# A graph layer's projection on raw rows, its weights loaded by other queues, six row groups instead of five, and a bias added behind the attention

## The chip, the cores and the metric

The kernel runs on one core of a Trainium2 chip, as one program and one launch. A core has five engines with their own instruction queues: TensorE (PE; its loads of the stationary operand are shown as PEld), VectorE (DVE), ScalarE (ACT), GpSimd (POOL) and SyncE (SP). SP, ACT and POOL also issue DMAs. Each engine takes its instructions in order; engines wait for each other by semaphores. The metric is the device time in microseconds, from start to end of the program on the core.

## The reference, cut to what matters

Two layers, each a graph attention over 3327 nodes followed by a feed-forward part. Layer 0's feed-forward part is a mixture of 16 experts of which each row takes two; layer 1's is 30 recurrent steps. The change concerns layer 0's graph attention with 2 heads of 128 features:

```python
x = x + L0_gnn(layernorm(x), adj, W1, b1, W2, b2, W3, b3, a)
x = x + L0_experts(layernorm(x), ...)          # top 2 of 16 experts
x = x + L1_gnn(layernorm(x), adj, W, a)        # one head of 256, elu
x = x + L1_recurrent(layernorm(x), ...)        # 30 steps

def L0_gnn(h, adj, W1, b1, W2, b2, W3, b3, a):
    W1h, W2h, W3h = h @ W1.T + b1, h @ W2.T + b2, h @ W3.T + b3     # (n, 2, 128)
    s1, s2 = W1h . a[:, :128], W2h . a[:, 128:]                     # (n, 2)
    e = leaky_relu(s1[:, None] + s2[None, :], 0.2)
    att = softmax(where(adj == 1, e, -9e15), axis=1)
    return att @ W3h                                                # per head
```

## The kernel before, in words

**State and tiles.** x lies in SBUF as 26 tiles of 128 rows by 256 features for the whole program. Lines 94 and 95 load it with SP in groups of 4 tiles. The adjacency is kept as bytes, turned (`adjT`): the column tile's 128 nodes lie on the partitions, the rows along the free axis.

**Taking the graph.** `take_graph` (L286) does that for one group of rows: POOL issues a DMA that casts the group's int32 rows to bytes in DRAM (`in_bytes`, L301), and SP issues one transposing DMA per tile into `adjT` (L311). There is one `in_bytes` buffer of 6 tiles, so the next group's cast waits until the transposes before it have read it.

**Projection of layer 0** (L387 to L456). POOL loads W1, W2, the attention vectors `aT`, the three biases and W3 (L400, L412), in this order. Sixteen one-column matmul records (L415) turn W1 and W2 with `aT` into four extra columns of the weight `wv`, which is 256 + 4 columns wide, so that one product gives the features and the scores. `project` (L151) then goes over the rows in groups of 4 tiles: statistics on VectorE (`inverse`, L109: bn_stats, bn_aggr), 1/sqrt on POOL (L120), normalised rows `xn` on VectorE (L127), four transposes for two tiles on TensorE (L147) with a copy to SBUF on ScalarE (L148), and the products of the two tiles before (L162). `split0` (L433) adds b3 to the features and a constant to the scores on VectorE; `Scores.finish` (L193) takes exponentials of the scores on ScalarE. Layer 1 calls the same function with raw rows: the mean is taken out of the weights (`without_mean`, L132) and 1/sigma is applied to the product (`split1`, L923).

**Attention** (`attend`, L201). For each group of rows, for each of 2 heads, for each of the 26 column tiles j: ScalarE makes `e` (L252) for all rows of the group, VectorE adds and multiplies with the mask into `pT` (L257), and TensorE adds one product for each row tile to `acc` (L262). `e` and `pT` have three buffers each. The row factors `rb` of the next part are made half way (L221, L225). The groups of rows are `groups0` (L45). When a group's head is done, `close` divides by the sum and adds into x (L235, L479) in small steps, one for each j of the next part. After the second head the generator `route` (L486) follows in the same way: normalise the group's rows into `row` (L490), store them, multiply with the gate, find the best two experts and their places, and queue the tokens' scattered DMAs (`list_tokens`, L565), each of which may also start the graph for a later group (L578). After the third group `find_tiles` (L631) finds which rows the first 16 slots of the experts work on.

**Experts.** `work_off` (L797) runs 61 slots; each loads an expert's weights by SP and gathers 128 rows by POOL. The routing of the last group runs beside the first slots.

**Order.** The framework's scheduler plans the order of each engine's queue when the program is built, from the order of the code and the dependencies; the transposes of `row` thus stand at a fixed place in TensorE's queue between products of the attention. `tc.issue_after` and `tc.keep_in_program_order` tie instructions to others.

Of the kernel before, what the change touches and what calls it, by code (L numbers as in the profile page):

```python
# [20 lines left out]
P = 128  # L21
# [4 lines left out]
G = 4  # L26
# [4 lines left out]
def gat_moe_gat_recurrent_ffn(ctx: ExitStack, tc: tile.TileContext, a: dict, out: bass.AP):  # L31
# [12 lines left out]
    groups = [range(t, min(t + G, NT)) for t in range(0, NT, G)]  # L44
    groups0 = [range(0, 4), range(4, 10), range(10, 16), range(16, 22), range(22, 26)]  # L45
    groups1 = [range(max(t - 2, 0), t + 2) for t in range(0, NT, G)]
# [46 lines left out]

    for ts in groups:
        move_pairs(a["x"], x[:, ts[0] : ts[-1] + 1, :], ts[0] // 2, (ts[-1] + 1) // 2, False)

# [35 lines left out]
    def without_mean(wv, n_out, ones, p):  # L132

        for k in range(KD):
            nc.tensor.matmul(p[:, :n_out], lhsT=ones, rhs=wv[:, k, :], start=(k == 0), stop=(k == KD - 1))
        for k in range(KD):
            nc.vector.scalar_tensor_tensor(
                wv[:, k, :], p[:, :n_out], -1.0 / D, wv[:, k, :], op0=ALU.mult, op1=ALU.add
            )

    def turned(two, work, ps):
# [8 lines left out]

    def project(groups, wv, n_out, finish, work, ps, ps_p, aside, raw=True):  # L151

        pending = None

        def products(hT, t, r):
            for j in range(2):
                p = ps_p()  # L160
                for k in range(KD):
                    nc.tensor.matmul(  # L162
                        p[:, :n_out], lhsT=hT[:, j, k, :], rhs=wv[:, k, :], start=(k == 0), stop=(k == KD - 1)
                    )
                finish(t + j, p, *([r[:, j : j + 1]] if raw else []))

        for ts in groups:
            n = len(ts)
            tiles = [x[:, t, :] for t in ts]
            if raw:  # L170
                r, _, power = inverse(tiles)
            else:
                xn = work.tile([P, G, D], F32, name="xn")
                power = normalized(tiles, [xn[:, j, :] for j in range(n)])
            aside(ts, power)
            for j0 in range(0, n, 2):
                hT = turned(x[:, ts[j0] : ts[j0] + 2, :] if raw else xn[:, j0 : j0 + 2, :], work, ps)
                if pending:
                    products(*pending)
                pending = hT, ts[j0], r[:, j0 : j0 + 2] if raw else None  # L180
        products(*pending)

    class Scores:


        def __init__(self, pool, heads, s=None):
            self.s = pool.tile([P, NT, 2, heads], F32, name="s") if s is None else s
            self.row = pool.tile([P, NT, heads], F32, name="row")
            self.full = pool.tile([P, NT, heads], F32, name="full")
            self.part = pool.tile([P, NT, heads], F32, name="part")  # L190
            self.minus = pool.tile([P, NT, heads], F32, name="minus")

        def finish(self, t0, t1):  # L193
            nc.scalar.activation(self.full[:, t0:t1], self.s[:, t0:t1, 1], AF.Exp)
            nc.scalar.activation(self.part[:, t0:t1], self.s[:, t0:t1, 1], AF.Exp, scale=ALPHA)
            nc.scalar.activation(self.row[:, t0:t1], self.s[:, t0:t1, 0], AF.Exp, scale=1.0 - ALPHA)
            nc.vector.tensor_scalar(self.minus[:, t0:t1], self.part[:, t0:t1], -1.0, None, op0=ALU.mult)
# [133 lines left out]
    lb = rec.tile([P, KD], F32, name="lb")  # L331
    fb = rec.tile([P, D], F32, name="fb")
    ones_r = rec.tile([P, P], F32, name="ones_r")
# [24 lines left out]
    with ExitStack() as moe:  # L358
# [19 lines left out]
        wh = keep.tile([P, NT, H, C + 1], F32, name="wh")  # L378
        sc = Scores(keep, H)
        ps = moe.enter_context(tc.tile_pool(name="ps0", bufs=4, space=PSUM))  # L380
# [6 lines left out]
        with ExitStack() as pre:  # L387
            work = pre.enter_context(tc.tile_pool(name="work0", bufs=2))
            hold = pre.enter_context(tc.tile_pool(name="hold0", bufs=1))

            zero = hold.tile([P, E * CAP * 2 // P], F32, name="zero")
            nc.vector.memset(zero, 0.0)
            nc.scalar.dma_start(lists.rearrange("(p n) k -> p (n k)", p=P), zero)
            for k in range(2):
                nc.scalar.dma_start(given[k * NP + N : (k + 1) * NP, :], zero[: NP - N, :D])
            nc.scalar.dma_start(no_row, zero[:2, : NP // 4])

            def once(name, shape, src):
                t = hold.tile(shape, F32, name=name)
                nc.gpsimd.dma_start(t, src)  # L400
                return t

            w1 = once("gw1", [P, H, D], a["W1"].rearrange("(h c) d -> c h d", c=P))
            w2 = once("gw2", [P, H, D], a["W2"].rearrange("(h c) d -> c h d", c=P))
            aT = once("gaT", [P, 2, H], a["aT"].rearrange("(s c) h -> c s h", c=P))
            b1 = once("gb1", [P, H], a["b1"])
            b2 = once("gb2", [P, H], a["b2"])
            b3 = once("gb3", [P, D], every_partition(a["b3"], D))


            wv = hold.tile([P, KD, D + 2 * H], F32, name="wv")
            nc.gpsimd.dma_start(wv[:, :, :D], a["W3T"].rearrange("(k p) c -> p k c", p=P))  # L412
            pv = bank()
# [7 lines left out]
            )  # L421
            shift = hold.tile([P, 2, H], F32, name="shift")
            nc.vector.memset(shift, 0.0)
            pv = bank()
            for h in range(H):
                for s, b in ((0, b1), (1, b2)):
# [3 lines left out]
                    )  # L430
            nc.vector.tensor_copy(shift[:, 0, :], pv[:, :H])

            def split0(t, p):  # L433
                nc.vector.tensor_tensor(
                    wh[:, t, :, :C], p[:, :D].rearrange("p (h c) -> p h c", h=H),
                    b3.rearrange("p (h c) -> p h c", h=H), ALU.add,
                )
                nc.vector.tensor_tensor(
                    sc.s[:, t], p[:, D : D + 2 * H].rearrange("p (s h) -> p s h", h=H), shift, ALU.add
                )  # L440
                if t % G == G - 1 or t == NT - 1:
                    sc.finish(t - t % G, t + 1)
# [5 lines left out]
            def first_rows(ts, power):  # L448
                nonlocal behind
                behind = power  # L450
                if ts is groups[3]:
                    take_graph(groups0[0], behind)

            project(groups, wv, D + 2 * H, split0, work, ps, bank, first_rows, False)
            nc.vector.tensor_scalar(wh[:, NT - 1], wh[:, NT - 1], real[:, 0:1], None, op0=ALU.mult)
# [30 lines left out]
        def route(ts):  # L486

            n, t0 = len(ts), ts[0]
            whole = [P, n, E]
            normalized([x[:, t, :] for t in ts], [row[:, j, :] for j in range(n)])  # L490
            here = slice(t0 * P, (t0 + n) * P)
# [72 lines left out]
            def list_tokens(j, t, s, behind):  # L564
                put = nc.gpsimd.indirect_dma_start(  # L565
                    out=lists, out_offset=bass.IndirectOffsetOnAxis(ap=ati[: rows(t), s, j : j + 1], axis=0),
                    in_=pair[: rows(t), t, s, :], in_offset=None,
                )
                tc.declare_no_dep(put.ins, group="places", reason="no two tokens have the same place in the lists")
                tc.add_to_no_dep_group("places", put.ins)  # L570
                if behind:

                    tc.add_manual_dep(
                        put.ins, behind.name,
                        mybir.DependencyInfo(mybir.DependencyClass.Sync, mybir.DependencyReason.DATA),
                        reason="spread over the columns",
                    )
                if (t, s) == (ts[-1], 1) and groups0.index(ts) < 2:  # L578
                    take_graph(groups0[groups0.index(ts) + 3], put.ins)

            for j, t in enumerate(ts):
                for s in range(2):
                    later.append(partial(list_tokens, j, t, s))
            if ts is groups0[2]:
                pieces = begin_tiles()

                def piece(behind):
                    if next(pieces, pieces) is not pieces:
                        later.appendleft(piece)

                quick.append(piece)
                later.append(piece)
# [4 lines left out]
        FIRST = 16  # L597
        EARLY = groups0[2][-1] + 1
        assert EARLY < NT - 1 and (2 * P * EARLY - E * (P - 1)) / P >= FIRST
# [271 lines left out]
        wc = rec.tile([P, KD, D], F32, name="wc")  # L871
        bb = rec.tile([P, D], F32, name="bb")
        wv1 = rec.tile([P, KD, D + 2], F32, name="wv1")
        va = rec.tile([P, 2, D], F32, name="va")
# [204 lines left out]
```

The softmax here doesn't subtract the row's maximum and nothing guards it: scores larger than these inputs give would overflow.

## Time and profile before

| | us |
|---|---|
| median of 3 runs | 2000.29 (1998.33 to 2000.75) |
| the profiled execution | 2004.62 |
| its span | 2002.9 |
| TensorE busy (matmul / weight load) | 1930.9 / 1750.0 |
| VectorE, ScalarE, GpSimd busy | 1299.7, 1095.5, 938.4 |

The span falls into five stages by the lines that run on TensorE: loads and layer 0's projection (0 to 53.3 us), its attention (53.3 to 395), the experts (to about 750), layer 1's projection and attention (to about 1100), and the recurrent steps. The page's groups show how often the lines of this change run: the attention's products (L262) leave 2704 records of 128x129 in layer 0 and 1352 of 128x257 in layer 1, the e and pT operations 494 each over both layers, 260 of them in layer 0. A busy TensorE in the profile is not TensorE at its peak, since the ends of matmuls are modelled; counts of records in equal windows are the better measure.

### The profile page before, as it was taken

The page shows a single profiled execution, that of the slowest core. Times are in us where ns is not written, and L with a number is a line of the kernel's source. Part 1 is how long each engine was busy: PE and PEld are TensorE (multiplying, and loading weights), DVE is VectorE, ACT ScalarE, POOL GpSimd, SP SyncE. Part 2 cuts the span into 40 slices and gives each one's busy share as a digit, 9 for nine tenths or more (in the row PEclk, how much of TensorE's full clock was granted, in tenths as well). Part 3 has the DMA queues.
Part 4 walks back from the last instruction along what each step waited for, and adds up shares of the span by engine and source line. Part 5 has one row for each costly group of instructions (what it writes and reads, how often), then busy time and mean ns, then how long its engine had stood idle before and what let it go on. Part 6 is the DMA issues. An engine that isn't in the chain of part 4 may idle for free.

```text
span 2002.9 us, 33524 instructions
## 1 busy us (share of the span) xinstructions
PE 1930.9 (96%) x12032; PEld 1750.0 (87%) x12032; DVE 1299.7 (65%) x3827; ACT 1095.5 (55%) x1419; POOL 938.4 (47%) x864
## 2 busy tenths in 40 slices
PE   7999999999999997999999999999999999999998
PEld 6999999989999986888888888888888888888887
DVE  6887888722222226567576777777777777777777
ACT  2967766621111115566555666666666666666664
POOL 3020212443333321001000787787787787787785
PEclk9999999999999998999999999999999999999999
DMA  8978141189999854000001000000000000000003
GB/s 165 119 100 119 10 76 50 39 291 324 351 330 308 297 195 137 9 8 17 9 17 35 1 1 1 1 1 1 1 1 1 1 1 1 1 1 1 1 1 116
DMA packets 139754, 157.08 MB, mean 78 GB/s; under 512 B 52027, under 2 KB 99364, under 8 KB 139586
## 3 DMA queue, kind: packets, MB, share of 16 engines
q1 hardware_dynamic: 123466, 122.05, 19.8%
q0 software_dynamic: 11440, 28.09, 8.1%
q10 hardware_dynamic: 4680, 4.76, 0.7%
q8 instruction: 98, 1.61, 0.3%
q14 instruction: 70, 0.57, 0.1%
HBM read 164.58 MB, written 29.78 MB: 97 GB/s over the span
## 4 chain that ended last, share of the span: by engine, by line
PE 68%; issue 9%; ACT 5%; POOL 5%; DVE 4%; DMA 3%; SPq 0%; another core or an unknown queue 0%; POOLq 0%; DVEq 0%; ACTq 0%
PE po L1014 35%; PE acc L262 23%; PE pt L1008 5%; ACT zT L1010 5%; DVE pT L257 2%; POOL given L831 2%; POOL rb L730 2%; DMA given<-wh,to 2%; PE bank L786 2%; PE acc L827 1%; PE bank L499 1%; PE bank L221 0%; DVE x L913 0%; PE acc L162 0%; POOL rstd L120 0%
## 5 line engine op out<-in xcount | busy, mean ns | idle before, releaser
L1014 PE MATMUL po<-wc,zT 128*128 128x256 f32 x3120 | 705.5, 383 | 21.7 <-ACT zT L1010 21.1
L1014 PEld LDWEIGHTS po<-wc,zT 128*128 128x128 f32 x3120 | 583.1, 190 | 124.1 <-ACT zT L1010 49.7
L252 ACT ACTIVATE e<-rb,minus,full 128x384 f32<-128x384 f32 (+3 forms) x494 | 400.2, 824 | 180.9 <-DVE pT L257 162.7
L1000 POOL TENSOR_TENSOR th<-th,x 128x1024 f32<-128x1024 f32 (+1 forms) x210 | 460.8, 2213 | 64.3 <-ACT th L998 62.7
L257 DVE SCALAR_TENSOR_TENSOR pT<-e,part,adjT 128x384 f32<-128x384 f32 (+3 forms) x494 | 381.1, 776 | 138.1 <-PE acc L262 117.5
L1019 DVE SCALAR_TENSOR_TENSOR x<-po,rr,bb 128x256 f32<-128x256 f32 x780 | 324.9, 478 | 118.3 <-PE po L1014 113.8
L1010 ACT COPY zT<-pt 128x1024 f32<-128x1024 f32 (+1 forms) x210 | 199.0, 947 | 334.0 <-PE pt L1008 334.0
L1006 DVE BATCH_NORM_STATS2 stats<-z 128x6 f32<-128x256 f32 x780 | 283.7, 415 | 117.6 <-ACT z L1001 117.6
L262 PE MATMUL acc<-wh,pT 128*128 128x129 f32 x2704 | 310.4, 276 | 1.8 <-DVE pT L257 1.8
L262 PEld LDWEIGHTS acc<-wh,pT 128*128 128x128 f32 x2704 | 305.2, 192 | 2.5 <-DVE pT L257 2.4
L262 PE MATMUL acc<-s_wh,pT 128*128 128x257 f32 x1352 | 295.3, 380 | 0.8 <-DVE pT L257 0.7
L262 PEld LDWEIGHTS acc<-s_wh,pT 128*128 128x128 f32 x1352 | 255.9, 190 | 37.7 <-DVE pT L257 1.8
L120 POOL TENSOR_TENSOR rstd<-ve,neg_half 128x4 f32<-128x4 f32 (+3 forms) x28 | 30.4, 1086 | 415.7 <-DVE ve L118 332.1
L989 POOL TENSOR_TENSOR rr<-rr,neg_half 128x4 f32<-128x4 f32 (+1 forms) x210 | 208.0, 990 | 17.4
L1001 ACT ACTIVATE z<-th 128x1024 f32<-128x1024 f32 (+1 forms) x210 | 210.6, 1003 | 0.6 <-POOL th L1000 0.5
L998 ACT ACTIVATE th<-x 128x1024 f32<-128x1024 f32 (+1 forms) x210 | 199.3, 995 | 1.9 <-DVE x L127 0.9
L1008 PE MATMUL pt<-ident,z 128*128 128x128 f32 x1560 | 191.6, 274 | 2.5 <-DVE high L944 2.5
L1008 PEld LDWEIGHTS pt<-ident,z 128*128 128x128 f32 x1560 | 179.5, 142 | 14.9 <-issue 2.9
L786 PEld LDWEIGHTS bank<-hT,wh 128*128 128x128 f32 x1280 | 150.7, 194 | 9.2 <-issue 4.8
L786 PE MATMUL bank<-hT,wh 128*128 128x128 f32 x1280 | 151.8, 277 | 6.6 <-issue 2.2
L820 DVE TENSOR_TENSOR pT<-e,bank 128x512 f32<-128x512 f32 x61 | 41.9, 687 | 176.9 <-PE bank L786 124.2
L816 ACT ACTIVATE e<-bank 128x512 f32<-128x512 f32 x61 | 36.4, 597 | 194.1 <-PE bank L786 90.3
(189 smaller groups left out, 1346.4 us busy)
## 6 DMA issues: line engine op xcount, KB each, us to landing
wh<-in_w_dram SPq DMA_DIRECT2D x120, 512.0 KB
first_set<-in_w_dram SPq DMA_DIRECT2D x63, 512.0 KB
in_bytes<-in_adj_dram POOLq DMA_DIRECT2D x3, 2496.0 KB
x<-in_x_dram SPq DMA_DIRECT2D x6, 512.0 KB
kept<-x SPq DMA_DIRECT2D x8, 384.0 KB
old<-kept SPq DMA_DIRECT2D x6, 512.0 KB
out_dram<-x SPq DMA_DIRECT2D x6, 512.0 KB
table_x<-row ACTq DMA_DIRECT2D x3, 768.0 KB
```

The costliest lines, as they stand in the source:

```text
L252: nc.scalar.activation(e[:, : n * P], rb[:, : n * P], AF.Relu, scale=sc.full[:, j, h : h + 1], bias=sc.minus[:, j, h : h + 1],)
L257: masked = nc.vector.scalar_tensor_tensor(pT[:, : n * P], e[:, : n * P], sc.part[:, j, h : h + 1], adjT[:, j // 2, ts[0] * P : (ts[-1] + 1 ...
L262: nc.tensor.matmul(po[c], lhsT=pT[:, c * P : (c + 1) * P], rhs=wh[:, j, h, :], start=(j == 0 and c % per_bank == 0), stop=(j == NT - 1), s ...
L786: nc.tensor.matmul(p[:, f, :], lhsT=w[:, k, f * P : (f + 1) * P], rhs=hT[:, k, :], start=(k == 0), stop=(k == KD - 1),)
L989: nc.gpsimd.tensor_tensor(r[:, :n], r[:, :n], neg_half[:, :n], ALU.pow)
L1000: nc.gpsimd.tensor_tensor(th[:, :n, :], th[:, :n, :], hs, ALU.add)
L1001: nc.scalar.activation(z[:, :n, :], th[:, :n, :], AF.Silu, scale=1.0 / S)
L1006: nc.vector.bn_stats(stats[:, j, :], z[:, j, :])
L1008: nc.tensor.transpose(pt[:, j, k, :], z[:, j, k * P : (k + 1) * P], ident)
L1010: nc.scalar.copy(zT[:, :n, :, :], pt[:, :n, :, :])
L1014: nc.tensor.matmul(po[:, j, :], lhsT=zT[:, j, k, :], rhs=wc[:, k, :], start=(k == 0), stop=(k == KD - 1),)
L1019: nc.vector.scalar_tensor_tensor(x[:, ts[0] + j, :], po[:, j, :], rr[:, j : j + 1], bb, op0=ALU.mult, op1=ALU.add)
```

## The change

1. Loads. SP loads the first group of x, then W3 into `wv`, then the rest of x. ACT loads W1 and W2, POOL `aT`, b1, b2 and b3. The zeros for DRAM follow on ACT.
2. Projection on raw rows. `without_mean` takes the mean out of `wv` (260 columns). The normalised copy goes away. `split0` scales the features by 1/sigma on ScalarE and the scores on VectorE. The statistics of the third group and later are issued after the weight is ready.
3. The constant of the scores goes into the exponential's bias, one ScalarE operation for each head.
4. b3 is added to x in `route`, for a whole group at once, behind the attention (the softmax weights add up to one). The `fb` buffer of layer 1 is allocated later under the same name.
5. Row groups of 2, 4, 6, 6, 4, 4 tiles instead of 4, 6, 6, 6, 4. The graph of the first group is asked for after the third group's statistics, not the fourth's. The early tiles of the experts are found after the fourth group (18 tiles of rows) instead of the third (16).

```diff
-    groups0 = [range(0, 4), range(4, 10), range(10, 16), range(16, 22), range(22, 26)]
+    groups0 = [range(0, 2), range(2, 6), range(6, 12), range(12, 18), range(18, 22), range(22, 26)]
...
-    for ts in groups:
-        move_pairs(a["x"], x[:, ts[0] : ts[-1] + 1, :], ts[0] // 2, (ts[-1] + 1) // 2, False)
+    def load_rows(some):
+        for ts in some:
+            move_pairs(a["x"], x[:, ts[0] : ts[-1] + 1, :], ts[0] // 2, (ts[-1] + 1) // 2, False)
+
+    load_rows(groups[:1])
...
         for ts in groups:
-            n = len(ts)
-            tiles = [x[:, t, :] for t in ts]
-            if raw:
-                r, _, power = inverse(tiles)
-            else:
-                xn = work.tile([P, G, D], F32, name="xn")
-                power = normalized(tiles, [xn[:, j, :] for j in range(n)])
+            with tc.issue_after(matrix) if matrix and ts not in groups[:2] else ExitStack():
+                r, _, power = inverse([x[:, t, :] for t in ts])
             aside(ts, power)
...
-            nc.scalar.activation(self.row[:, t0:t1], self.s[:, t0:t1, 0], AF.Exp, scale=1.0 - ALPHA)
+            if self.shift is None:
+                nc.scalar.activation(self.row[:, t0:t1], self.s[:, t0:t1, 0], AF.Exp, scale=1.0 - ALPHA)
+            else:
+                for h in range(self.row.shape[2]):
+                    nc.scalar.activation(
+                        self.row[:, t0:t1, h], self.s[:, t0:t1, 0, h], AF.Exp,
+                        scale=1.0 - ALPHA, bias=self.shift[:, h : h + 1],
+                    )
...
+            def once(engine, name, shape, src):
+                t = hold.tile(shape, F32, name=name)
+                tc.keep_in_program_order(engine.dma_start(t, src))
+                return t
+            wv = hold.tile([P, KD, D + 2 * H], F32, name="wv")
+            nc.sync.dma_start(wv[:, :, :D], a["W3T"].rearrange("(k p) c -> p k c", p=P))
+            load_rows(groups[1:])
+            w1 = once(nc.scalar, "gw1", [P, H, D], a["W1"].rearrange("(h c) d -> c h d", c=P))
+            w2 = once(nc.scalar, "gw2", [P, H, D], a["W2"].rearrange("(h c) d -> c h d", c=P))
+            aT = once(nc.gpsimd, "gaT", [P, 2, H], a["aT"].rearrange("(s c) h -> c s h", c=P))
...
-            w1 = once("gw1", [P, H, D], a["W1"].rearrange("(h c) d -> c h d", c=P))
-            w2 = once("gw2", [P, H, D], a["W2"].rearrange("(h c) d -> c h d", c=P))
-            aT = once("gaT", [P, 2, H], a["aT"].rearrange("(s c) h -> c s h", c=P))
...
+            nc.vector.tensor_scalar(shift, pv[:, :H], 1.0 - ALPHA, None, op0=ALU.mult)
+            matrix = without_mean(wv, D + 2 * H, ones, bank())
+
+            def split0(t, p, r):
+                nc.scalar.activation(
+                    wh[:, t, :, :C], p[:, :D].rearrange("p (h c) -> p h c", h=H), AF.Copy, scale=r
+                )
+                nc.vector.tensor_scalar(
+                    sc.s[:, t], p[:, D : D + 2 * H].rearrange("p (s h) -> p s h", h=H), r, None, op0=ALU.mult
                 )
...
-                if ts is groups[3]:
+                if ts is groups[2]:
                     take_graph(groups0[0], behind)
 
-            project(groups, wv, D + 2 * H, split0, work, ps, bank, first_rows, False)
+            project(groups, wv, D + 2 * H, split0, work, ps, bank, first_rows, matrix)
...
+            mine = x[:, t0 : t0 + n, :]
+            nc.vector.tensor_tensor(mine, mine, b3[:, None, :].to_broadcast([P, n, D]), ALU.add)
             normalized([x[:, t, :] for t in ts], [row[:, j, :] for j in range(n)])
...
-                if (t, s) == (ts[-1], 1) and groups0.index(ts) < 2:
+                if (t, s) == (ts[-1], 1) and groups0.index(ts) < len(groups0) - 3:
...
-            if ts is groups0[2]:
+            if ts is groups0[-3]:
                 pieces = begin_tiles()
...
-        EARLY = groups0[2][-1] + 1
+        EARLY = groups0[-3][-1] + 1
```

## The prediction

> **What bounds the kernel now.** I read the table of windows first, then the timelines of TensorE and of the queues at the start, then the boundaries between row groups. In the windows (start:end, length, then busy time and instructions of PE, PEld, DVE, ACT and POOL) a full 20 us of layer 0's attention holds 181 matmul records, 20/181.3 = 0.1103 us each. A fp32 product of 128 columns leaves two records, so one tile of rows costs 2 x 0.1103 = 0.22 us per column tile.
>
> ```profile
> 60.00:80.00 20.00, 20.00 (x181) 20.00 (x180) 17.36 (x28) 18.37 (x26) 0.00 (x0) 1.00 0.87 104
> ...
> 180.00:200.00 20.00, 18.68 (x167) 18.26 (x165) 16.43 (x38) 12.45 (x15) 1.99 (x1) 1.00 0.71 143
> ...
> 340.00:360.00 20.00, 17.32 (x152) 16.77 (x151) 14.50 (x44) 11.75 (x16) 3.66 (x3) 1.00 0.22 74
> ```
>
> TensorE sets the pace except at the boundaries (167 and 152 records), and before the first product. The start, on TensorE:
>
> ```profile
> 11.83 3.55 PE L415 MATMUL bank<-gaT,gw 128*128 128x1 f32 x16 [11.83 <-DMA gaT<-in_aT_dram]
> ...
> 20.95 3.22 PE L162 MATMUL bank<-wv,hT 128*128 128x260 f32 x8
> ...
> 46.36 3.67 PE L162 MATMUL bank<-wv,hT 128*128 128x260 f32 x16
> ...
> 53.32 12.88 PE L262 MATMUL acc<-wh,pT 128*128 128x129 f32 x113 [0.16 <-DVE pT L257]
> ```
>
> It waits 11.83 us for aT, the projection's products run from 20.95 to 50.03, and attention begins at 53.32. It ends at 395.27, where the experts' first product starts. So there are two terms: when attention begins, and what it loses after that. The graph does not limit either (POOL issues the byte copies, SP the transposes):
>
> ```profile
> 17.93 0.91 POOL L301 DMA_DIRECT2D in_bytes<-in_adj_dram  x1
> ...
> 48.49 0.77 POOL L301 DMA_DIRECT2D in_bytes<-in_adj_dram  x1 [17.17 <-DMA adjT<-in_bytes]
> ...
> 91.19 0.69 POOL L301 DMA_DIRECT2D in_bytes<-in_adj_dram  x1 [41.93 <-DMA adjT<-in_bytes]
> ```
>
> A group of 4 tiles takes 48.49 - 17.93 = 30.6 us from its issue to the end of its transposes, one of 6 takes 42.7; hence 6.05 us a tile plus 6.4, and 18.5 for 2 tiles.
>
> **What the Trainium skill says.** "DMA: Bandwidth & Descriptors", section "Issuing engines are not separate DMA queues": all queues share 16 engines, and another queue saves only issue time. The trace agrees that they share (the DMA share is 1.0 from 7 to 15 us), so I expect the weights earlier because they stand ahead of x, not because of the queue as such. "TensorE: Matmul & The Clock Gate", "What's actually happening": half clock until about 3.4 us of sustained work. The trace fits: the first eight products take 3.22 us, later eights 1.92. "VectorE: DVE Perf Modes", "The TRN2 errata": a fp32 tensor_tensor takes (N+151)/0.96 ns, 1224 for N = 1024; layer 1's 128x1024 adds (L913) measure 1215 to 1220.
>
> **The start.** Durations are from one execution of 2004.62 us (span 2002.9), 4.3 above the median 2000.29; I work out a difference and apply it to the median. The first x group (512 KB), W1, W2 (512) and W3 (256) now stand ahead: 1.28 MB, at the 0.24 to 0.31 MB/us of the windows from 2 to 7 us, is down by 6.7 us. aT goes first on POOL's queue instead of after 512 KB; I take 5.5 us for it and W1 (no earlier than 4.5, the first x group's landing before; no later than 11.8). The 16 products on aT (3.55 us) end near 9. The planned order puts the second x group's statistics (4 x 0.4 us) ahead of the copy of the score vectors on VectorE, and that group lands near 9.3, so the copy comes at 11.0. Then the added work of without_mean: two products and three bias products on TensorE, 2.2 us at mixed clock, and two 128x260 operations of 0.42 us on VectorE. First product: 14.3 (bounds 12.3 and 16.3) in place of 20.95. Thirteen pairs follow at the old pace, 2.19 us for four transposes and eight records, less two transposes done in the wait: 13 x 1.62 + 11 x 0.57 = 27.4. ScalarE's two scaled copies a pair (0.48 each, as layer 1's L924, 128x258) and its hT copy (0.58) make 1.5 us and stay under 2.19; VectorE loses its 26 xn operations (0.41) and adds (0.42), which were hidden. The last product ends at 41.9, before 50.03: -8.1. The tail to the first acc (3.3 us) keeps its chain; I take -8.0 in all (bounds -6 and -10).
>
> The first byte copy is issued after the third group's statistics, about 17 us as before; its 2 tiles are ready at 35, the next 4 at 66, needed at 72. Six us in hand; the next 6 tiles at 109, needed near 123.
>
> **What attention pays.** (1) Group of 2 tiles: TensorE needs 2 x 0.2206 = 0.44 us per column tile, but ScalarE cannot follow:
>
> ```profile
> 51.67 1.52 ACT L252 ACTIVATE e<-rb,minus,full 128x512 f32<-128x512 f32 x2
> 52.39 1.50 ACT L252 ACTIVATE e<-rb,minus,full 128x512 f32<-128x512 f32 x2
> ...
> L252 ACT ACTIVATE e<-rb,minus,full 128x256 f32<-128x256 f32 x26 | 15.3, 599 | 9.4 <-DVE pT L257 8.1 <-DVE mv L116 0.9
> ```
>
> The first e operations start 0.71 us apart at 0.81 each (512 elements), 0.1 less than they last. At 256 they last 0.60 (layer 1's last group), so 0.50 apart: 52 x 0.50 + 0.8 for the rb copies = 26.8, against 22.9 on TensorE. Cost +3.9 (2.5 to 5).
>
> (2) L221's products that fill the tail before attention fall from 28 records to 16; the 12 come later: 12 x 0.11 = +1.3.
>
> (3) The add of b3, once a group, before the statistics. At boundaries VectorE and the chain after it are late already (start, length):
>
> ```profile
> 192.78 2.03 DVE L127 TENSOR_SCALAR row<-x,mv,rstd 128x256 f32<-128x256 f32 x6 [1.25 <-POOL rstd L120]
> ...
> 193.34 0.67 PE L147 MATMUL bank<-ident,row 128*128 128x128 f32 x4 [1.32 <-DVE row L127]
> ...
> 348.88 2.05 PE L262 MATMUL acc<-wh,pT 128*128 128x129 f32 x16 [1.50 <-DVE pT L257]
> ```
>
> TensorE stands at its transposes of row, so a longer chain adds idle time unless the plan moves them back. Adds of 2, 4, 6, 6, 4 tiles: 0.69 + 1.22 + 1.76 + 1.76 + 1.22 = 6.65 us. In the planned order the transposes after the group of 4 move from column tile 8.3 to 9.8, which hides that add; those of the 6 under 6 move only from 10.5 to 10.8. I count 0.6 + 0.2 + 1.3 + 1.5 + 1.2 = +4.8 (0 to 6.65). The last group's add lies in the experts' stage, where VectorE is busy 4 to 8 of 20 us: nothing.
>
> (4) Boundaries. TensorE's own work is the same 22 routed tiles, so only idle time changes. From the spans of the groups less their records times 0.11 I get some 2.3 us idle for 4 under 6 and 6 under 6, 6 for 6 under 4. One 6 under 6 goes; 2 under 4 and 4 under 4 come. VectorE's routing of 4 tiles is 3 us less than of 6 (statistics, row, gate operations), so 4 under 4 is 3, and 2 under 4 about 1: +1.7 (0 to 4). (5) find_tiles moves from a group of 6 to one of 4, with less room on VectorE (0.67 of 0.88 us): +0.5 (-1 to 2).
>
> The experts' stage keeps 61 slots and its order, with 18 tiles of tokens for the first 16 slots; its entry I put at nothing, 2 us either way.
>
> Sum: -8.0 + 3.9 + 1.3 + 4.8 + 1.7 + 0.5 = +4.2; 2000.3 + 4.2 = 2004.5 us.
>
> **Rivals.** Not slower: the chain at the boundaries covers the adds and the extra boundary. It can, for TensorE idles there on POOL's rstd (1.25 us) and VectorE has gaps later in each group. Place: the first 12 column tiles of a group; price 4.8 + 1.7 + 0.5 = 7.0; it decides when over 4.2 of that is covered. Then -8.0 to -10 with 5.2 of (1) and (2) left: 1996.5. Against: VectorE's list from 177.65 to 190.5 us shows no gap.
>
> Slower still: the start gains little. If aT or the score copy is as late as before, first product at 18.5 and 2.4 gained: +9.8, 2010. For: small-element transfers on POOL's queue landed 8 us after issue. Against: they stood behind 512 KB.
>
> No effect: the byte copies and transposes of the graph limit the earlier attention at its second or third group; over 6 us late they eat the gain and no more is lost elsewhere: about 2000.
>
> **Numbers.** Likeliest, 2004.5 (own range 2000.5 to 2008.5): 0.46, of which 0.34 slower by over 0.2% (4 us, about what a measurement can tell from no change) and 0.12 within. Covered boundaries: 0.38, of which 0.28 faster, 0.10 within. Little gained: 0.11, slower. No effect: 0.05, 0.03 within and 0.02 faster. Faster 0.30, within 0.25, slower 0.45. With cases on both sides the range is 1994.5 to 2010.
>
> **What would show it.** First projection product at 14 us, first acc at 45; e operations back to back at 0.50 us and TensorE with holes until 72; idle time before L151's transposes about 1.5 us longer for groups of 6; experts' stage from 399. Wrong if attention begins after 48, if a pT waits for a transpose, or if the boundaries' idle time does not grow.

## The result, and the profile after

The changed kernel takes 2019.65 us (median of 4 runs, 2016.5 to 2021.15); the kernel before took 1999.31 beside it. The ratio is 1.0089, 95% interval 1.0076 to 1.0102: some 18 to 20 us slower. The forecast was 2004.5, so the sign was right, and the loss was four to five times the 4.2 us that the sum gave. The profiled execution took 2016.5 us (span 2014.8), the lowest of the four, while the one of before (2004.62) lay above its median; the difference between these two profiles is therefore 11.9 us, where the medians differ by 20.3.

The same three windows that the prediction showed, in the profile after (busy time and instructions of PE, PEld, DVE, ACT and POOL, then the granted clock, the DMA share and GB/s):

```profile
60.00:80.00 20.00, 19.63 (x160) 18.91 (x160) 19.07 (x45) 20.00 (x38) 0.68 (x1) 1.00 0.84 124
180.00:200.00 20.00, 20.00 (x181) 20.00 (x180) 14.21 (x14) 15.04 (x17) 0.00 (x0) 1.00 0.90 110
340.00:360.00 20.00, 15.96 (x97) 15.61 (x96) 10.18 (x40) 7.43 (x10) 6.28 (x6) 0.74 0.38 108
```

At 60 to 80 ScalarE is busy all the time and TensorE gets 160 records: the group of 2 tiles. Between boundaries the old pace stands, 181. From 340 to 360 TensorE gets 97 records, with a mean clock of 0.74. No stretch of 20 us in the attention before has fewer than 146. The start, on TensorE:

```profile
8.89 3.57 PE L427 MATMUL bank<-gaT,gw 128*128 128x1 f32 x16 [8.89 <-DMA gaT<-in_aT_dram]
...
17.64 2.48 PE L166 MATMUL bank<-wv,hT 128*128 128x260 f32 x8
...
42.31 3.67 PE L166 MATMUL bank<-wv,hT 128*128 128x260 f32 x16
...
48.57 13.61 PE L270 MATMUL acc<-wh,pT 128*128 128x129 f32 x107 [0.80 <-PE bank L229]
```

The first product comes at 17.64 instead of 20.95 and the first acc at 48.57 instead of 53.32. A gain, but of 4.75 us, not 8.0. A boundary, group of 6 after 6: VectorE (the add, then row behind POOL's rstd), and TensorE at the same place:

```profile
213.15 1.75 DVE L501 TENSOR_TENSOR x<-x,fb 128x1536 f32<-128x1536 f32 x1
...
222.30 2.03 DVE L130 TENSOR_SCALAR row<-x,mv,rstd 128x256 f32<-128x256 f32 x6 [1.26 <-POOL rstd L123]
```
```profile
219.10 2.72 PE L270 MATMUL acc<-wh,pT 128*128 128x129 f32 x22 [1.61 <-DVE pT L265]
222.86 0.67 PE L151 MATMUL bank<-ident,row 128*128 128x128 f32 x4 [1.04 <-DVE row L130]
```

TensorE waited 1.32 us at such a boundary before. Now it waits twice, 1.61 us for a pT that VectorE computes behind the add and the statistics, and 1.04 us for row. And the stretch from 340 to 360, on TensorE and in windows of 4 us:

```profile
344.68 1.38 PE L270 MATMUL acc<-wh,pT 128*128 128x129 f32 x10
349.89 0.58 PE L723 MATMUL bank<-va,row 104*128 104x16 f32 x2 [3.83 <-DMA row<-lists]
...
352.17 2.16 PE L723 MATMUL bank<-va,row 104*128 104x16 f32 x10
354.16 8.04 PE L270 MATMUL acc<-wh,pT 128*128 128x129 f32 x45
```
```profile
344.00:348.00 4.00, 2.06 (x16) 1.84 (x16) 2.38 (x11) 1.81 (x3) 0.00 (x0) 1.00 0.23 70
348.00:352.00 4.00, 2.11 (x10) 2.14 (x11) 0.00 (x0) 0.00 (x0) 0.00 (x0) 0.71 0.99 235
352.00:356.00 4.00, 4.00 (x20) 4.00 (x20) 1.25 (x7) 0.77 (x1) 0.00 (x0) 0.50 0.54 196
356.00:360.00 4.00, 4.00 (x21) 4.00 (x20) 2.90 (x9) 1.67 (x3) 3.32 (x3) 0.51 0.14 38
```

TensorE stands 3.83 us at the products that build the first part of the experts' tile table (L723): the token lists, which they read back from DRAM, have not landed. When it goes on, its clock is half for 10 us: 45 acc records take 8.04 us instead of 5.0. The Trainium skill, "TensorE: Matmul & The Clock Gate", section "What's actually happening", says the clock falls to half after an idle window of about 3.4 us; this trace agrees (3.83 us idle, then 0.50), though waits well under 3.4 us were followed by it too (see the last section). Wait and half clock together cost 8.9 us: 3.83 idle, and 4 x (0.29 + 0.50 + 0.49) = 5.1 that the granted clock lost in the three windows from 348 to 360. (The expectations below still count 9.6.)

**A ledger of the attention.** VectorE reads the sums of a finished half (one head of one row group) with a reciprocal for each tile (L235 before, L243 after); the starts of the first reciprocals in VectorE's timeline cut layer 0's attention into halves. The first half of a group carries the routing of the group before it. Subtracting 26 column tiles times the group's tiles times 0.2206 us leaves the excess of each half. Summed by kind, in us (the kernel before from its own run e8 below; the columns with 298.2 us at TensorE's pace give the last row within 1 us):

| excess over TensorE's pace | before | after | after, b3 in the projection (e5) | before, groups only (e7) | after, old groups (e2) |
|---|---|---|---|---|---|
| first group, both halves | 1.9 | 3.7 | 3.7 | 3.4 | 1.9 |
| other first halves (boundaries) | 31.8 | 41.2 | 34.7 | 39.6 | 38.6 |
| the half in which the table is built | 4.8 | 12.9 | 8.8 | 12.9 | 4.8 |
| other second halves | 4.4 | 7.3 | 8.1 | 7.5 | 4.4 |
| first to last acc, by the records | 341.1 | 363.1 | 353.4 | 361.5 | 347.1 |

Of the 22.0 us that the attention lost, 9.3 lie at boundaries, 8.0 in the half with the table, 1.8 in the first group, 2.9 in other second halves (from values before rounding). The start gives 4.7 back, so attention ends 17.4 us later.

A loss can be counted in the half after the one that causes it. The half with the table ends at 355.4, but the half clock lasts to 359.9, so it costs the boundary that follows about 2.2 us. That boundary has an excess of 8.9 in the changed kernel and of 6.8 in e4, a run with the same groups and adds whose clock stays full there. Counted where they arise, some 10 of the 22 us belong to the table and some 7 to the boundaries.

### The profile page after: what moved, and what is told of

The parts are those of the page before. It is cut to its first block, busy times and chain, and to the rows that moved or that the text cites. A ratio compares the mean times of both kernels' runs of the same rounds, so it can differ in the third digit from the quotient of the medians.

```text
span 2014.8 us, 33680 instructions
## 1 busy us (share of the span) xinstructions
PE 1943.0 (96%) x12040; PEld 1759.2 (87%) x12040; DVE 1304.7 (65%) x3858; ACT 1123.2 (56%) x1505; POOL 938.9 (47%) x863
## 3 DMA queue, kind: packets, MB, share of 16 engines
q8 instruction: 98, 1.61, 0.3%
## 4 chain that ended last, share of the span: by engine, by line
PE 80%; ACT 6%; DVE 5%; issue 4%; DMA 3%; POOL 2%; SPq 0%; POOLq 0%; DVEq 0%; ACTq 0%
PE po L1027 35%; PE acc L270 24%; PE bank L798 7%; PE pt L1021 5%; ACT zT L1023 5%; PE acc L839 3%; DVE pT L265 3%; ACT e L260 2%; DMA given<-wh,to 1%; PE bank L166 1%; PE bank L151 1%; PE bank L229 1%; POOL given L843 1%; DMA lists<-pair,ati 1%; POOL rb L742 1%
## 5 line engine op out<-in xcount | busy, mean ns | idle before, releaser
L260 ACT ACTIVATE e<-rb,minus,full 128x384 f32<-128x384 f32 (+3 forms) x546 | 414.2, 780 | 185.3 <-DVE pT L265 168.1
L265 DVE SCALAR_TENSOR_TENSOR pT<-e,part,adjT 128x384 f32<-128x384 f32 (+3 forms) x546 | 390.9, 721 | 130.2 <-PE acc L270 112.2
L270 PE MATMUL acc<-wh,pT 128*128 128x129 f32 x2704 | 320.0, 279 | 8.3 <-DVE pT L265 7.2
L270 PEld LDWEIGHTS acc<-wh,pT 128*128 128x128 f32 x2704 | 312.7, 194 | 11.2 <-DVE pT L265 9.8
L1002 POOL TENSOR_TENSOR rr<-rr,neg_half 128x4 f32<-128x4 f32 (+1 forms) x210 | 208.0, 991 | 17.4
L832 DVE TENSOR_TENSOR pT<-e,bank 128x512 f32<-128x512 f32 x61 | 41.9, 687 | 162.9 <-PE bank L798 159.3
```

The source lines that it names most:

```text
L260: nc.scalar.activation(e[:, : n * P], rb[:, : n * P], AF.Relu, scale=sc.full[:, j, h : h + 1], bias=sc.minus[:, j, h : h + 1],)
L265: masked = nc.vector.scalar_tensor_tensor(pT[:, : n * P], e[:, : n * P], sc.part[:, j, h : h + 1], adjT[:, j // 2, ts[0] * P : (ts[-1] + 1 ...
L270: nc.tensor.matmul(po[c], lhsT=pT[:, c * P : (c + 1) * P], rhs=wh[:, j, h, :], start=(j == 0 and c % per_bank == 0), stop=(j == NT - 1), s ...
L1002: nc.gpsimd.tensor_tensor(r[:, :n], r[:, :n], neg_half[:, :n], ALU.pow)
```

## The experiments

Each ratio is against the kernel before, run beside it on the same chip; its median there was 2004.06 for e1 to e4, 2005.54 for e5 to e8 and 2006.32 for e9 and e10. In these runs 0.001 is 2 us.

**e1: the table under a group of 6.**

```diff
-    groups0 = [range(0, 2), range(2, 6), range(6, 12), range(12, 18), range(18, 22), range(22, 26)]
+    groups0 = [range(0, 2), range(2, 6), range(6, 10), range(10, 16), range(16, 22), range(22, 26)]
```

> Row groups of 2, 4, 4, 6, 6, 4 tiles instead of 2, 4, 6, 6, 4, 4: still six groups and the same neighbours (2 before 4, 4 before 6, 6 before 6, 6 before 4, 4 before 4 once each), but the tile table is built under a group of 6 tiles, as before the change. Theory A (in the changed kernel TensorE reaches the table's products before the lists are read back, stands 3.8 us and then runs at half clock, 9.6 us in all): 9 to 10 us faster than the changed kernel, 2010, with no wait of L723 on row and the granted clock at 1.0 there. Theory B (the sixth group and its boundary are what cost): unchanged, 2018 to 2021. The forecast's own term for this move, 0.5 us: 2019.

Measured: 1.0062 (1.0048 to 1.0075), some 5 us less than the changed kernel, between the two. Theory A's place is right: the lists are read at 334.22 and the products follow at 346.07 with no wait and at full clock, and that half takes 39.2 us as in the kernel before. But part of the gain is lost earlier: in the second head of the second group of 4 TensorE waits 1.68 us for pT and then runs 3.4 us at half clock, and that half takes 31.2 us where the group of 4 in the changed kernel took 25.8. Why pT is late there stays open (see e10).

**e2: the row groups of before.** The one edit is the list of groups, back to 4, 6, 6, 6, 4.

> The changed kernel with the row groups of before (4, 6, 6, 6, 4); raw rows, loads on other queues and the add behind the attention stay. Theory A: the table's wait goes (-9.6), and with the group of 2 (-3.6), L229's products in the attention (-1.3) and one boundary (-1): 2004. What is left against the kernel before would be the start, 4.75 us earlier, and the adds, about 5 us later: within 3 us of 1999.3 to 2004. Theory C (the changed projection or the adds cost more than that): 2008 or more.

Measured: 1.0046 (1.0032 to 1.0059). The attention falls from 363.1 to 347.1 us: groups and table cost 16.0 there. What remains above the 341.1 of before is 6.0, and the boundaries alone have 6.8 more (38.6 against 31.8), about the 6.5 us that the adds of the four groups last: these are the adds. The first acc comes only at 51.7, since the graph's first four tiles are late now:

```profile
50.87 5.51 DVE L265 SCALAR_TENSOR_TENSOR pT<-e,part,adjT 128x512 f32<-128x512 f32 x7 [2.24 <-DMA adjT<-in_bytes]
```

The byte copy is issued at 20.58 instead of 17.93, because the third group's statistics now wait for the weights; with the first group of 2 tiles this did not show. Between the profiles of e2 and e8 attention and start make 4.5 us, and the experts' stage, which took 404.0 us from last acc to layer 1's first against 401.2, another 2.8. The profiled execution of e2 was the fastest of its five; what the 9 us between medians hold beyond this was not seen.

**e3: b3 added on GpSimd instead.**

```diff
                 behind = take_graph(ts, behind)
+                if ts is groups0[1]:
+                    for four in groups:
+                        mine = x[:, four[0] : four[-1] + 1, :]
+                        with tc.issue_after(behind):
+                            nc.gpsimd.tensor_tensor(mine, mine, b3[:, None, :].to_broadcast([P, len(four), D]), ALU.add)
...
-            mine = x[:, t0 : t0 + n, :]
-            nc.vector.tensor_tensor(mine, mine, b3[:, None, :].to_broadcast([P, n, D]), ALU.add)
```

> The changed kernel with the add of b3 done on GpSimd while the first groups attend (seven additions of up to 128x1024 behind the second byte copy), none on VectorE at the boundaries. The forecast's step 3: 4.8 us faster, 2015, idle time before the transposes of row shorter by 0.2 to 1.5 us a group; the add's full length on the path: 6.7 us, 2013. Rival (the chain covers the adds): unchanged, 2019 to 2020. With the wait for the lists untouched neither removes more than 7 us, unless the routing that comes earlier by 1.8 us shortens that wait too; then up to 10.

Measured: 1.0125 (1.0109 to 1.0140), slower than the changed kernel, which neither theory held possible. The timelines of GpSimd, VectorE and TensorE:

```profile
40.40 13.85 POOL L472 TENSOR_TENSOR x<-x,fb 128x1024 f32<-128x1024 f32 x6
```
```profile
41.32 12.97 DVE L205 TENSOR_SCALAR minus<-part 128x8 f32<-128x8 f32 x1 [0.58 <-ACT part L196]
```
```profile
54.46 5.37 PE L166 MATMUL bank<-wv,hT 128*128 128x260 f32 x12 [10.99 <-DVE s L448]
```

An operation of VectorE on 8 columns, 0.17 us elsewhere, took 12.97 us while GpSimd did six of its seven additions, and TensorE stood 10.99 us in the middle of the projection for what is queued behind it. The Trainium skill, "SBUF — State Buffer", section "SBUF: two separate sides", says that the two engines share a port pair as an exclusive lock held for a whole instruction; the trace fits (VectorE ends at 54.29, GpSimd's sixth addition at 54.25). If it is this lock, it was not given over between six instructions; no run here tests another cause. Behind this the attention is shorter by 7.3 us than in the changed kernel (355.8 from first to last acc), as it is in e5 below, where the adds leave the boundaries too.

**e4: TensorE kept busy through the wait.**

```diff
-            pw = bank()[:, : 2 * n].rearrange("p (k s) -> p k s", k=2)
+            pw = bank()
+            if not s0:
+                for _ in range(16):
+                    nc.tensor.matmul(pw[:, 256 : 256 + P], lhsT=ones, rhs=ones, start=True, stop=True)
+            pw = pw[:, : 2 * n].rearrange("p (k s) -> p k s", k=2)
```

> The changed kernel with 16 products of ones on ones (128x128, some 3.5 us, nobody reads them) set ahead of the 16 products that build the tile table (L723), so that TensorE is not idle while it waits for the lists. If the half clock after that wait comes of TensorE's idle time: no clock under 0.9 between 345 and 362 us, and 5 to 6 us of the 9.6 come back, 2014. If the clock falls for another reason: half clock stays, unchanged at 2019 to 2020. If the added products themselves delay the attention: 2022.

Measured: 1.0080 (1.0066 to 1.0094). The clock answers the first question. Windows of e4:

```profile
348.00:352.00 4.00, 3.75 (x33) 3.75 (x34) 2.04 (x12) 1.38 (x2) 0.00 (x0) 1.00 0.47 100
352.00:356.00 4.00, 4.00 (x37) 4.00 (x36) 1.24 (x6) 0.00 (x0) 0.17 (x1) 1.00 1.00 358
356.00:360.00 4.00, 4.00 (x38) 4.00 (x37) 3.94 (x14) 3.45 (x5) 3.29 (x3) 1.00 0.29 86
```

The half clock is gone when TensorE is not idle, and 37 and 38 records stand where 20 and 21 stood. So the half clock came of TensorE's idle time. The time came back only in part: 1.8 us from the table's first product at L652 to the end of the half after it, and the attention as a whole is no shorter (363.6). The planned order now puts the table's products ahead of five more acc products, and VectorE's chain before them is exposed: TensorE waits 0.94, 0.66, 0.67 and 0.52 us in it.

**e5: b3 added in the projection.**

```diff
-                nc.scalar.activation(
-                    wh[:, t, :, :C], p[:, :D].rearrange("p (h c) -> p h c", h=H), AF.Copy, scale=r
-                )
+                nc.vector.scalar_tensor_tensor(
+                    wh[:, t, :, :C], p[:, :D].rearrange("p (h c) -> p h c", h=H), r,
+                    b3.rearrange("p (h c) -> p h c", h=H), op0=ALU.mult, op1=ALU.add,
+                )
...
-            mine = x[:, t0 : t0 + n, :]
-            nc.vector.tensor_tensor(mine, mine, b3[:, None, :].to_broadcast([P, n, D]), ALU.add)
```

> The changed kernel with b3 added in the projection, by one VectorE operation a tile (product times row's factor plus b3) in place of ScalarE's scaled copy, and no add at the boundaries. The runs so far put the adds at 5.4 us (attention of 347.1 us with the groups of before against 341.7 without adds). If the adds are paid in full at the boundaries: 5 to 6 us less than the changed kernel, ratio 1.006 to before. If shorter routing also brings the lists before the table's products: up to 10 less, 1.004. Rival (the chain's slack covers them): as the changed kernel, 1.009. If VectorE now limits the projection: first acc later than 50 us and little gained.

Measured: 1.0059 (1.0041 to 1.0077), some 6 us less than the changed kernel; the attention falls by 9.7 us to 353.4. First acc at 48.7, so VectorE does not limit the projection. Two terms went at once: the boundaries lost 6.5 us of excess (the adds, and the half clock), and the table's wait is gone:

```profile
339.73 0.35 SPq L647 DMA_DIRECT2D row<-lists  x1
```
```profile
344.23 0.38 PE L722 MATMUL bank<-va,row 104*128 104x16 f32 x2
```

The missing adds alone do not explain that, for e7 below has none either, and waits. Counted from the start of the half, the first list write comes after 4.1 us in both; but the read goes out after 23.8 us in e5 and 26.0 in e7, since two of e7's later writes and the landing of the last took longer, and TensorE is at the products after 28.3 us in e5 and 26.7 in e7, mainly since in e5 it has waited 1.7 us for VectorE on the way. The lists need about 4.2 us. With a margin this small, small delays decide. Even without the wait the half keeps 4.0 of the 8.0 us.

**e6: the start.** The groups of before, and:

```diff
+            aT = once(nc.scalar, "gaT", [P, 2, H], a["aT"].rearrange("(s c) h -> c s h", c=P))
             w1 = once(nc.scalar, "gw1", [P, H, D], a["W1"].rearrange("(h c) d -> c h d", c=P))
             w2 = once(nc.scalar, "gw2", [P, H, D], a["W2"].rearrange("(h c) d -> c h d", c=P))
-            aT = once(nc.gpsimd, "gaT", [P, 2, H], a["aT"].rearrange("(s c) h -> c s h", c=P))
...
-                if ts is groups[2]:
+                if ts is groups[1]:
```

> The changed kernel with the groups of before, aT as the first load on ScalarE's queue instead of GpSimd's, and the first byte copy of the graph one group of statistics earlier. If aT's 7.2 us from issue to landing come of GpSimd's queue: aT there by 6 us, first product 14.5 to 15.5, first acc 47 to 49 us, 3 to 4 us less than the same kernel without these two edits (ratio 1.0046): 1.0028. If they come of the 16 shared engines being full: first product stays at 17 to 18, first acc 50.4 (only the 1.2 us wait for adjT goes), 1.004.

Measured: 1.0028 (1.0018 to 1.0037), but not for the expected reason: first product at 19.04 and first acc at 51.9, no earlier than in e2; the attention is that of e2 (347.3), and of the 3.6 us less by the ratio 2.7 lie behind it, where the experts' stage took 401.3 instead of 404.0. On TensorE, then on VectorE:

```profile
6.36 1.84 PE L427 MATMUL bank<-gaT,gw 128*128 128x1 f32 x8 [6.36 <-DMA gw<-in_W_dram]
9.99 1.86 PE L427 MATMUL bank<-gaT,gw 128*128 128x1 f32 x8 [1.79 <-DMA gw<-in_W_dram]
```
```profile
18.35 0.14 DVE L637 COPY vec<-part 16x1 f32<-16x1 f32 x1 [3.22 <-POOL part L474]
...
18.48 0.74 DVE L140 SCALAR_TENSOR_TENSOR wv<-bank,wv 128x260 f32<-128x260 f32 x2
```

With aT ahead on another queue, TensorE waits for W1 until 6.36 and for W2 until 9.99: aT is no longer the limit, the weights are, and the 16 products end 0.5 us earlier than in e2. The first product is later all the same (17.92 in e2). In the planned order VectorE's subtraction of the mean from wv stands behind small operations on `part`, which GpSimd writes after the byte copy that this edit moved forward, and VectorE waits 3.22 us for it. So neither of the two expectations was tested cleanly: what aT's queue alone is worth stays open.

**e7: nothing but the groups**, in the kernel before: the new list of groups, and the three places that count them (`len(groups0) - 3`, `groups0[-3]` twice).

> The kernel before with nothing but the six row groups (2, 4, 6, 6, 4, 4 tiles) and what hangs on their numbers: projection, loads and b3 as before. From the runs so far six groups cost 11.6 us in the attention, the place of the table 4.4, and bring the first acc 1 to 2 us earlier: 13 to 15 us slower than before, ratio 1.007. The forecast's terms for the groups (3.9 + 1.3 + 1.7 + 0.5 = 7.4 us): 1.0037. If short groups hurt only together with the adds: below 1.003.

Measured: 1.0087 (1.0068 to 1.0105). The groups alone make the kernel as slow as the whole change does, but with other terms: it has no earlier start (first acc 53.4) and no adds, and yet its boundaries lose nearly as much as those of the whole change (39.6 against 41.2; 34.7 in e5). Most of that is the clock: at two boundaries TensorE runs 3.4 us at half clock, and each is 1.6 us longer than in e5; a third, behind the table's half, is 1.0 longer. That the two sums agree is chance. The wait is there without any add:

```profile
PE bank L711 <- DMA row<-lists: 3.6, 1, 3.6
```

**e8: the kernel before again**, without an edit, for its profile beside e5 to e7.

> The kernel before itself, on the chip of these runs, for its profile: attention 341 to 343 us from first to last acc, experts' stage 401 to 404 us; ratio 1.000 within 0.001.

Measured: 0.9994 (0.9985 to 1.0002); attention 341.1, experts' stage 401.2 us.

**e9: what is left without groups and adds.** The groups of before, b3 in the projection as in e5, the first byte copy one group earlier as in e6.

> The changed kernel with the groups of before, b3 added in the projection by VectorE, and the first byte copy of the graph one group of statistics earlier: what is left of the change is raw rows and the loads. If the adds were 6 us and the groups the rest: attention back at 341 to 343 us, first acc 50 to 51, 2 to 3 us faster than before (ratio 0.9985). If the changed projection costs something of its own: no faster than before.

Measured: 0.9988 (0.9981 to 0.9994), 2.8 us faster than before: the one version that beats both. First acc at 50.3, 2.9 earlier than in e8, attention 343.3. Of the 2.2 us by which this is longer than in e8, nearly 2 lie at the first boundary, where this execution ran 3.4 us at half clock (from 111.5).

**e10: only the groups, with the table under 6 tiles**: e7 with the list of groups of e1.

> The kernel before with six row groups in the order 2, 4, 4, 6, 6, 4 (and what hangs on their numbers): the table is built under 6 tiles. Against the same kernel with 2, 4, 6, 6, 4, 4 (1.0087): if the place of the table is 8 to 9 us of that, no wait of its products on row and 1.0045; what stays then is the group of 2 and one boundary. If the place hardly matters (forecast: 0.5 us): 1.0085.

Measured: 1.0065 (1.0051 to 1.0080), 4.4 us less than e7. The attention is 7.3 us shorter (354.2 against 361.5) and the wait for the lists is gone; the half with the table takes 39.2 us. As in e1 the second group of 4 has lost time, 3.12 us of waiting for a pT and then half clock. What pT waited for there the profile names only "remote", while the DMA engines were idle and GpSimd wrote lists; this stays open. With the table under 6 tiles the wait for the lists is gone with the adds (e1) and without them (e10).

## Why the forecast was right or wrong

- **The start (-8.0): right in kind, 3.3 us too large.** The term that failed is "I take 5.5 us for it and W1": aT was there at 8.89. Everything after it held: 5.3 us were forecast from the end of the 16 products to the first projection product, and 5.2 were measured; the projection then ran at 2.19 us a pair. The trace of before showed aT at 11.83 - 3.35 = 8.5 us from issue, behind 512 KB on its queue, and I put that down to the queue. After, with nothing ahead of it, it took 7.2. The Trainium skill, "DMA: Bandwidth & Descriptors", section "Issuing engines are not separate DMA queues", which the prediction itself cited, says that DMAs of all queues interleave on the same 16 engines; the trace agrees in that a free queue of its own brought only 1.3 us (8.5 to 7.2). But in e6, issued 0.8 us sooner on ScalarE's queue, aT was there within 5.6 us, so where and when it is issued was not without effect. By the prediction's own sign (wrong if attention begins after 48) this term failed: 48.57. A slip in its sum changes nothing: 14.3 + 13 x 1.62 + 11 x 0.57 is 41.6, not 41.9.
- **The group of 2 (+3.9): right.** It took 26.6 us (26.8 forecast), with ScalarE's e operations 0.50 us apart, as shown by 14 of them:

```profile
59.44 6.98 ACT L260 ACTIVATE e<-rb,minus,full 128x256 f32<-128x256 f32 x14
```

  In the ledger it counts only 1.8, since the first group of before had 1.9 us of excess too, which the forecast left out.
- **L229's products (+1.3):** part of the 2.9 us in other second halves, not separated further.
- **The adds (+4.8): about right in size, wrong in place.** By boundary, after against e5, the difference is 0.1, 0.2, 1.8, 1.6 and 2.8 us, where the forecast had 0.6, 0.2, 1.3, 1.5 and 1.2. The last one follows the table's half, and 2.2 of its 2.8 are the half clock; that leaves some 4.3 us for the adds, the two early ones hidden. With the old groups (e2 against e8) they cost 6.8, about all of the 6.5 that they last. So the rival that the boundaries cover them falls for the late groups. The forecast looked for the loss at the transposes of row (L151). There TensorE's waits in the attention fell from 4.9 to 2.9 us in all; its waits for pT rose from 1.7 to 7.2 (in e5, without the adds, both are 4.8): a pT that stands behind the add delays TensorE before row is due.
- **The extra boundary and mix (+1.7):** 2.9 in the ledger (e5 against before).
- **The table moved (+0.5, bounds -1 to 2): this step failed.** It cost 8.0 us in its half and some 2.2 in the next. I counted VectorE's room under a group of 4 and not the chain of DMAs that has to fit under it: GpSimd issues twelve list writes, SP then reads all lists back, and TensorE's products near the end of the half need what was read. Before (here the run e8), each of the last writes waited for its column, and there was room to spare; after, GpSimd is the limit. First e8, then after; GpSimd, SP's read, and TensorE's first product:

```profile
316.83 0.96 POOL L565 DMA_INDIRECT lists<-pair,ati  x1 [1.72 <-DVE pT L257]
320.40 0.96 POOL L565 DMA_INDIRECT lists<-pair,ati  x1 [2.62 <-DVE pT L257]
...
322.62 0.36 SPq L636 DMA_DIRECT2D row<-lists  x1
...
334.48 0.31 PE L711 MATMUL bank<-va,row 104*128 104x16 f32 x2
```
```profile
339.54 1.46 POOL L577 DMA_INDIRECT lists<-pair,ati  x1 [0.30 <-DVE cnt L657]
341.31 1.00 POOL L577 DMA_INDIRECT lists<-pair,ati  x1 [0.31 <-issue]
342.61 0.95 POOL L577 DMA_INDIRECT lists<-pair,ati  x1 [0.30 <-DVE cnt L672]
...
345.67 0.36 SPq L648 DMA_DIRECT2D row<-lists  x1
```

  In e8 the writes end 1.3 us before the read at 322.62, and the products come 11.9 us after it (334.48). After, the twelve writes from 325.33 to 343.56 follow one another with 0.3 us between them, the read goes out at 345.67, and TensorE is at the products at 346.06: the half has only 26 columns of 0.88 us instead of 1.32. The read landed about 4.2 us after its issue. What the forecast needed was in the trace of before (writes of 1.0 to 1.8 us, the read at 323.19, the products at 335.06). Of the loss, 3.83 us are the wait and 5.1 the half clock after it, which the forecast had not thought of at all; but e5, without both, still has 4.0 more in this half than before, of which 1.7 are waits for VectorE and the rest was not separated.
- **The experts' stage (0, 2 either way):** 396.3 us from last acc to layer 1's first acc in the profile after, 399.9 to 405.1 in ten other runs and 401.3 before. So that one execution gained 5 us there; the change does not reliably. Why this stage varies was not found.

The errors sum up: table 9.7 with the half clock that it leaves to the next half, start 3.3, other second halves 1.6, mix 1.2, adds -0.5, first group -2.1, together 13.2 of the 13.2 us by which the attention's end differs from the forecast (+17.4 against e8, where +4.2 was forecast). The rest up to the 20.3 us between medians lies after the attention, or between executions; the runs do not settle it.

## What to carry to other kernels

When a step is moved under a shorter piece of work, count the whole chain that has to fit beneath it, the queue that issues the small transfers and their landing included, and not the compute engines' room alone. A wait of TensorE of 3.8 us cost 8.9 us here, because half clock followed it. An elementwise add can be free inside a stage whose engine has slack (e5, e9) and cost up to its length when it is moved to a boundary (e2). When one edit takes a wait away, look at what else moved: in e5 it was not the edit alone, and in e6 a moved byte copy held up VectorE.

## What had not been expected of the hardware

- While GpSimd did six additions in a row, VectorE's 128x8 tensor_scalar took 12.97 us (0.17 us otherwise).
- Half clock, for 3.4 us at a time, also followed waits much shorter than 3.4 us, but not always: in e7 waits of 1.00 and 1.32 us at two boundaries (half clock from 146.9 and from 228.9), in e1 one of 1.68, in the changed kernel one of 1.79 (from 298.5); in e8 none of the waits of up to 1.4 us in the attention.
- A 2 KB transfer took 7.2 us from issue to landing as the first on its queue, with a mean DMA share of 0.92 from 2 to 9 us.
